# A two-layer graph network on one Trainium2 core: a shorter prelude, the last attention tiles side by side, and work of a step's start left for the next block

## The chip, the cores and the metric

The kernel runs on one core of a Trainium2 chip. The metric is the time on the device of one execution, in microseconds; three executions of the kernel before took 3805.06, 3805.78 and 3810.45 us, so the median is 3805.78 us. A profile is of one execution of its own. The engines are PE (matrix products and transposes through an identity, into PSUM), DVE (vector work), ACT (activations and most copies out of PSUM), POOL (elementwise work on SBUF, and here DMA issues too) and SP (which only issues DMAs). Each works through its own list of instructions in order and waits at semaphores for the others.

## What is computed

There are N = 2708 nodes with D = 512 features each, 22 tiles of up to 128 rows (the last has 20). Layer one is a graph attention with 8 heads of 64, layer two two steps of a diffusion with a "nucleus" attention. Cut to what matters:

```
h = relu(layernorm(x));  f = h W            # per head
e_self, e_neigh = f . a_self, f . a_neigh
attn = softmax(leaky(e_self[:,None] + e_neigh[None,:]) masked by adj)
x = x + relu(attn f + b)
X = relu(layernorm(x));  S = adj + I
for s in 0, 1:
    logits = (Xa W1) W2 (Xa W3)^T           # N x N
    A  = softmax(logits kept to the smallest set of largest terms with mass >= 0.9)
    Xf, Xb, Xa = Rf Xf, Rb Xb, A Xa         # Rf, Rb: S scaled by row, column sums
    Z += Xf U1[s] + Xb U2[s] + Xa U3[s]
x = x + layernorm(X + Z) gamma + beta
```

Since Rf and Rb are S with its rows scaled, the kernel multiplies by S and scales the result.

## The kernel before, in words

**Prelude** (lines 216 to 294). W, the attention vectors and the small weights are loaded; DVE forms `wa`, W times both attention vectors (L231, L232). Then a loop over 22 tiles: x is loaded (L254), normalised with `moments` (BN statistics on DVE, the power on POOL), centred on DVE (L257), clipped on POOL (L258), transposed on PE (L262), copied to `h_t` by ACT (L264). PE then forms `pe` (L270, 8 columns, e_neigh by node), `pr_t` (L273, e_self with heads as rows) and `pf` (L276, the features). ACT takes exponentials of them (L278 to L280), DVE writes the weighted features `fw` (L281). `r_t` holds e_self for all nodes and is written to DRAM (`en_d`, L284) at the end. The order of the instructions here and in layer one is made by a scheduler.

**Layer one** (L381 to L425). The nodes are cut into six chunks of 4, 4, 4, 4, 3 and 3 tiles. For each chunk and each group of four heads, over the 22 tiles of neighbours, DVE forms the attention terms `e` (L411) and PE accumulates them into `po` (L413). What remains for each tile of a chunk is a list of five stages (`finished`): `turned` (transposes of `o_t`), `shared` (division by the sums), `normed`, `cleared` (the second layer's normalised input, to `va_d`) and `asked` (its transposes, its split into a high and a low half, and its keys and queries to `kq_d`). These stages are put between the tiles of the next chunk's loop; those of the last chunk (tiles 19, 20, 21) come after it, tile after tile, in the order i*5+n (L420 to L425).

**The steps** (L883 on). The order on PE, ACT, DVE and SP is that of the source here; POOL's is the scheduler's. A step works on pairs of tiles, 11 blocks, with `g` from -1 to 10. Block g does four things at once:

- `search` finds for pair g+1 the threshold that keeps a mass of 0.9: rounds of passes over the 128 x 2708 exponentials on DVE (`mass`, L603), a choice (`choose`, L674 to L680), then `late()`, then `finish` (L779 on), which makes `keep` and ends with a branch (L863).
- `lg[g+2].products()` (L488) forms the logits of pair g+2 on PE; ACT copies them to `p` (L498). There are four buffers of `p`, so that of pair g+2 is free only when `finish` of pair g is done.
- `exp` (L501) is a list of steps on ACT, called fills: four exponentials over a whole row (L528, L535), on POOL the guesses (`points`, L538), twelve "looks" (L528, passes that count the mass above three guesses for each tile), and `masses` on POOL (L553), which the next search starts from.
- `late` runs, for pair g, `attended` (A Xa: transposes of `keep`, L983, copies `at`, L987, products L1002) and `mixed` (the products with U, L1030). Between their products `paced` places fills and "others".

The others (`part`, L913) are the products with S for four tiles (`product`, L938, with loads of `hl` and `s_r` by SP), and at their end `scaled`: ACT scales a result to `xe` (L944, two buffers), POOL writes it to `xfb_d`, and in step 0 DVE splits it in two halves (L181, L182) that POOL writes to DRAM too. `diffused` (L963) loads the scaled rows of pair g back.

In block -1 there is no pair to attend: `late` issues all fills, then all others, in that order, and only then does `finish` follow on DVE:

```
if g < 0:
    paced(fills, len(fills))
paced(others, len(others))
paced(fills, len(fills))
```

Of the kernel before, what the change touches and what calls it, by code (L numbers as in the profile page):

```python
# [9 lines left out]
F32 = mybir.dt.float32  # L10
# [14 lines left out]
P = 128  # L25
# [28 lines left out]
def kernel(  # L54
# [147 lines left out]
    with ExitStack() as l0:  # L202
# [13 lines left out]
        with tc.tile_pool(name="l0w", bufs=1) as wp, tc.tile_pool(name="l0p", bufs=2) as pp, \  # L216
                tc.tile_pool(name="l0ps", bufs=2, space=PSUM) as ps:
            w_sb = wp.tile([P, KD, D], F32, name="w_sb")
# [31 lines left out]
            r_t = wp.tile([H, N], F32, name="r_t")  # L250
            for t in range(NT):
                pr = rows[t]
                xt = pp.tile([P, D], F32, name="xt", bufs=3)
                nc.sync.dma_start(out=xt[:pr], in_=x[cols[t], :])  # L254
                h = pp.tile([P, D], F32, name="h")
                mean, rs = moments(pp, xt[:pr], pr)
                nc.vector.tensor_scalar(h[:pr], xt[:pr], mean, rs, op0=OP.subtract, op1=OP.mult)  # L257
                nc.gpsimd.tensor_scalar(h[:pr], h[:pr], 0.0, None, op0=OP.max)  # L258
                pt = ps.tile([P, KD, P], F32, name="tp")
                h_t = pp.tile([P, KD, P], F32, name="h_t")  # L260
                for k in range(KD):
                    nc.tensor.transpose(pt[:, k, :pr], h[:pr, k * P:(k + 1) * P], ident[:pr, :pr])  # L262
                for k in range(KD):
                    nc.scalar.activation(h_t[:, k, :pr], pt[:, k, :pr], AF.Copy,  # L264
                                         accum_out=hs[:, k, t:t + 1])
                pf = ps.tile([P, D], F32, name="pf")
                pe = ps.tile([P, H], F32, name="pe")
                pr_t = ps.tile([H, P], F32, name="pr_t")
                for k in range(KD):
                    nc.tensor.matmul(pe[:pr], lhsT=h_t[:, k, :pr], rhs=wa[:, k, H:],  # L270
                                     start=(k == 0), stop=(k == KD - 1))
                for k in range(KD):
                    nc.tensor.matmul(pr_t[:, :pr], lhsT=wa[:, k, :H], rhs=h_t[:, k, :pr],  # L273
                                     start=(k == 0), stop=(k == KD - 1))
                for k in range(KD):
                    nc.tensor.matmul(pf[:pr], lhsT=h_t[:, k, :pr], rhs=w_sb[:, k, :],  # L276
                                     start=(k == 0), stop=(k == KD - 1))
                nc.scalar.activation(fw[:pr, t, :, DH], pe[:pr], AF.Exp)  # L278
                nc.scalar.activation(kk[:pr, t, :], pe[:pr], AF.Exp, scale=-C)
                nc.scalar.activation(r_t[:, cols[t]], pr_t[:, :pr], AF.Exp, scale=C)  # L280
                nc.vector.tensor_mul(fw[:pr, t, :, :DH],  # L281
                                     pf[:pr].rearrange("p (h d) -> p h d", h=H),
                                     fw[:pr, t, :, DH:].to_broadcast([pr, H, DH]))
            nc.sync.dma_start(out=en_d, in_=r_t)  # L284
# [36 lines left out]
        def finished(t, o_t, c0):  # L321
# [5 lines left out]
            def turned():  # L327
                xt = work.tile([P, D], F32, name="xt0")
                nc.sync.dma_start(out=xt[:pr], in_=x[cols[t], :])
                held.append(xt)  # L330
                for g, grp in enumerate(hgroups):
                    pn = ps_t.tile([P, 512], F32, name=f"pn{g}")
                    pns.append(pn[:, :HG * DV].rearrange("p (h d) -> p h d", h=HG))
                    for i, hd in enumerate(grp):
                        nc.tensor.transpose(pns[g][:pr, i, :], o_t[:, hd, c0:c0 + pr], ident[:DV, :DV])

            def shared():
                den = small.tile([P, H], F32, name="den")
                rden = small.tile([P, H], F32, name="rden")
                o = work.tile([P, D], F32, name="o")  # L340
                held.append(o)
                o3 = o.rearrange("p (h d) -> p h d", h=H)
                for pn, grp in zip(pns, hgroups):
                    nc.vector.tensor_scalar(den[:pr, grp[0]:grp[-1] + 1], pn[:pr, :, DH],
                                            lone_n[:pr, t:t + 1], None, op0=OP.add)
                nc.vector.reciprocal(rden[:pr], den[:pr])
                for pn, grp in zip(pns, hgroups):
                    s = slice(grp[0], grp[-1] + 1)
                    nc.vector.scalar_tensor_tensor(o3[:pr, s, :], f3[:pr, s, :], lone[:pr, t:t + 1],
                                                   pn[:pr, :, :DH], op0=OP.mult, op1=OP.add)  # L350
                nc.gpsimd.tensor_mul(o3[:pr], o3[:pr], rden[:pr].unsqueeze(2).to_broadcast([pr, H, DH]))
                nc.gpsimd.tensor_add(o[:pr], o[:pr], b_b[:pr])
# [8 lines left out]
            def cleared():  # L361
                _, o, mean, rs = held
                v = work.tile([P, D], F32, name="v")
# [5 lines left out]
            def asked():  # L369
                v = held[4]  # L370
                pt = ps_t.tile([P, 512], F32, name="pn0").rearrange("p (k d) -> p k d", k=KD)
                for k in range(KD):
                    nc.tensor.transpose(pt[:, k, :pr], v[:pr, k * P:(k + 1) * P], ident[:pr, :pr])
                v_t = work.tile([P, KD, P], F32, name="v_t", bufs=1)
                nc.scalar.copy(v_t[:, :, :pr], pt[:, :, :pr])
                split_rows(halves, nc.gpsimd, v[:pr], t, vhl_d)
                project(halves, ps_t.tile([P, 512], F32, name="pn1"), v_t, t, 0)
# [4 lines left out]
        for ci, tiles in enumerate(tchunks):  # L382
# [22 lines left out]
            for grp, r_b in zip(hgroups, r_bs):  # L405
                po = [ps_o.tile([DV, 512], F32, name="po") for _ in grp]
# [12 lines left out]

            for i, t in enumerate(tiles):  # L420
                for n, stage in enumerate(finished(t, o_t, t * P - n0)):
                    later.setdefault(i * 5 + n, []).append(stage)
# [460 lines left out]
    for s in range(STEPS):  # L883
        last = s == STEPS - 1
        with ExitStack() as st:
# [28 lines left out]
            def part(half, b):  # L914
# [9 lines left out]
                if last or first:  # L924
                    half[:] = [ps_s.tile([P, D], F32, name=f"q{i}") for i in range(len(quad))]
# [4 lines left out]
                def product(c):  # L930
                    hl = sp.tile([P, 2, D], F32R, name="hl", bufs=3)
# [186 lines left out]
            with tc.manual_schedule(engines={PE, ACT, DVE, SP}):  # L1118
# [16 lines left out]
                ready = None  # L1135
                for g in range(-1, NP):

                    fills = []
                    if g + 2 < NP:
                        lg[g + 2].products()  # L1140
                    if g + 3 < NP:
# [4 lines left out]
                    others = part(half, g + 2)  # L1146
# [6 lines left out]
                    def late(g=g):  # L1153
                        if g >= 0:
                            keep, rden = ready
                            xf, xb = diffused(pairs[g])
                            xa, v_t = attended(pairs[g], keep, rden, fills, others, lambda: turned_rows(pairs[g], xf))
                            done.extend(mixed(pairs[g], v_t, xb, xa, others, fills))
                        elif last:
                            spread()  # L1160
                        if g < 0:
                            paced(fills, len(fills))
                        paced(others, len(others))
                        paced(fills, len(fills))
# [41 lines left out]
```

## Time and profile before

| what | us |
|---|---|
| median of three executions | 3805.78 |
| the profiled execution: its own time | 3807.19 |
| its span, first to last instruction | 3804.9 |
| prelude and the wait for layer one's first products | 0 to about 175 |
| layer one's loop | about 175 to 1082 |
| its last three tiles, to the first product of logits | 1082 to 1135 |
| step 0: block -1, blocks 0 to 10 | 1135 to 1293, to about 2400 |
| step 1: block -1, blocks 0 to 10 | about 2400 to 2569, to 3805 |

Over the span PE is busy 89%, DVE 69%, ACT 41% and POOL 22%; the mean granted TensorE clock is 0.957. Times in the text are microseconds from the start of the span. In an answer of the timeline, the columns are start, duration, engine, line, operation, output and inputs, a count where equal instructions were merged, and in brackets how long the engine had been idle and what it waited for. In the table by stretches each engine has its busy time and its number of instructions; the clock (1.00 is full speed), the DMA share and the DMA rate follow.

### The profile page before, as it was taken

To read this page: it belongs to the slowest core of one execution; us is meant where nothing else is said; L and a number is where in the kernel's file an instruction comes from. 1 tells how busy PE (TensorE), PEld (TensorE's weight loads), DVE (VectorE), ACT (ScalarE), POOL (GpSimd) and SP (SyncE) were. 2 spreads that over 40 slices of the span, in tenths; PEclk is the share of its full clock that TensorE was granted. 3 is DMA by queue.
4 is the path that set the end of the run, shared out by engine and by line. 5 is a ranking of instruction groups with operands and counts; after the bars stand their busy time and mean duration, and the time that the engine had idled before them with its cause. 6 is when DMAs were issued, how large, how long until landed. Compare 5 with 4: busy or idle time off the path is not lost. (4 is left out here: it accounts for less than half of the span.)

```text
span 3804.9 us, 35734 instructions
## 1 busy us (share of the span) xinstructions
PE 3402.3 (89%) x11313; PEld 1772.6 (47%) x11313; DVE 2611.5 (69%) x4814; ACT 1542.6 (41%) x2328; POOL 825.6 (22%) x1186
## 2 busy tenths in 40 slices
PE   7999999999955398999989899769999999999888
PEld 4433333333434254555555453445555665556442
DVE  3387888889945644545364642698779798777991
ACT  2234211111116255666656541256545556445511
POOL 3202331514331112121211211311121211211101
PEclk9999999999978699999999999989999999999999
DMA  2277434233226345453544543684566665567552
GB/s 75 80 265 260 156 99 139 82 106 108 82 66 234 135 147 191 152 203 113 198 153 152 188 153 97 224 291 164 188 209 220 228 211 190 198 208 245 182 204 70
DMA packets 276122, 634.09 MB, mean 167 GB/s; under 512 B 37033, under 2 KB 70097, under 8 KB 272899
## 3 DMA queue, kind: packets, MB, share of 16 engines
q1 hardware_dynamic: 248847, 540.99, 43.2%
q0 software_dynamic: 27024, 90.30, 6.2%
q8 instruction: 90, 1.47, 0.2%
q14 instruction: 161, 1.32, 0.1%
HBM read 509.07 MB, written 122.10 MB: 166 GB/s over the span
## 5 line engine op out<-in xcount | busy, mean ns | idle before, releaser
L1002 PE MATMUL a<-va,at 128*128 128x512 f32 (+2 forms) x1936 | 889.0, 598 | 10.2 <-ACT at L987 10.1
L938 PE MATMUL q<-hl,s_r 128*128 128x512 f32 x2904 | 824.2, 430 | 53.3 <-DMA s_r<-s_d 52.9
L413 PE MATMUL po<-e,fw 128*65 128x512 f32 (+4 forms) x2112 | 841.1, 554 | 29.9 <-DVE e L411 17.3
L411 DVE SCALAR_TENSOR_TENSOR e<-r_b,kk,a_c 128x512 f32<-128x512 f32 (+4 forms) x1056 | 752.5, 741 | 68.7 <-PE po L413 18.9
L938 PEld LDWEIGHTS q<-hl,s_r 128*128 128x128 f32 x2904 | 546.5, 190 | 298.7 <-issue 140.4
L528 ACT ACTIVATE junk_a<-p,nth 128x2708 uint8<-128x2708 f32 (+1 forms) x240 | 613.1, 2555 | 93.3 <-POOL nth L548 89.7
L413 PEld LDWEIGHTS po<-e,fw 128*65 128x65 f32 (+1 forms) x2112 | 286.4, 140 | 545.1 <-issue 272.9
L1002 PEld LDWEIGHTS a<-va,at 128*128 128x128 f32 (+2 forms) x1936 | 336.5, 186 | 374.0 <-issue 340.4
L1030 PE MATMUL a<-u_k,v_t 128*128 128x512 f32 (+1 forms) x1056 | 489.4, 599 | 23.1 <-ACT xa L1010 15.5
L603 DVE SCALAR_TENSOR_TENSOR junk<-p,th 128x2708 bf16<-128x2708 f32 (+1 forms) x132 | 402.3, 3048 | 4.0
L987 ACT COPY at<-t 128x512 f32<-128x512 f32 (+3 forms) x308 | 139.9, 475 | 440.9 <-PE t L983 440.5
L496 PE MATMUL t<-keys,q_t 128*128 128x452 f32 x528 | 168.1, 447 | 167.0 <-ACT p L498 155.0
L1030 PEld LDWEIGHTS a<-u_k,v_t 128*128 128x128 f32 (+1 forms) x1056 | 187.6, 186 | 242.0 <-issue 182.6
L779 DVE SCALAR_TENSOR_TENSOR keep<-p,th 128x2708 f32<-128x2708 f32 (+1 forms) x44 | 133.4, 3033 | 143.0 <-PE t L983 141.8
L181 DVE TENSOR_SCALAR split_hl<-xe 128x512 int32<-128x512 int32 (+1 forms) x44 | 19.0, 433 | 306.4 <-ACT xe L944 247.3
L496 PEld LDWEIGHTS t<-keys,q_t 128*128 128x128 f32 x528 | 92.6, 213 | 237.9 <-ACT p L498 208.0
L781 DVE MAX8 vn<-keep 128x8 f32<-128x2708 f32 (+1 forms) x66 | 196.8, 2981 | 2.3
L498 ACT COPY p<-t 128x452 f32<-128x452 f32 (+2 forms) x264 | 132.0, 539 | 144.0 <-DVEq L863 71.2
L395 ACT ACTIVATE s_c<-a_c 128x512 fp32r<-128x512 f32 (+3 forms) x132 | 76.2, 577 | 253.1 <-DMA a_c<-in_adj_t_dram 129.4
L983 PE MATMUL t<-ident,keep 128*128 128x128 f32 (+1 forms) x968 | 147.3, 274 | 24.3 <-DVE keep L731 16.6
L983 PEld LDWEIGHTS t<-ident,keep 128*128 128x128 f32 (+1 forms) x968 | 115.1, 139 | 104.2 <-issue 75.9
L523 DVE TENSOR_REDUCE nmx<-p 128x1 f32<-128x2708 f32 (+1 forms) x44 | 129.2, 2966 | 26.7 <-ACT p L498 26.7
(281 smaller groups left out, 3134.1 us busy)
## 6 DMA issues: line engine op xcount, KB each, us to landing
s_r<-s_d SPq DMA_DIRECT2D x330, 256.0 KB, 4.0
hl<-vhl_d SPq DMA_DIRECT2D x132, 512.0 KB, 4.0
u_k<-in_L_gnn_U_dram SPq DMA_DIRECT2D x264, 256.0 KB, 4.9
hl<-fhl_d SPq DMA_DIRECT2D x132, 512.0 KB, 5.3
hl<-bhl_d SPq DMA_DIRECT2D x132, 512.0 KB, 3.6
arow<-in_adj_dram SPq DMA_DIRECT2D x21, 1354.0 KB, 7.1
s_d<-s_c SPq DMA_DIRECT2D x88, 256.0 KB, 2.4
a_c<-in_adj_t_dram SPq DMA_DIRECT2D x84, 256.0 KB, 3.9
```

Of the source, the lines that this page charges most:

```text
L411: nc.vector.scalar_tensor_tensor(e[:pr, :cw], r_b[:pr, i, :cw], kk[:pr, t, hd:hd + 1], a_c[t][:pr, :cw], op0=OP.max, op1=OP.mult)
L413: nc.tensor.matmul(po[i][:, :cw], lhsT=fw[:pr, t, hd, :], rhs=e[:pr, :cw], start=(t == 0), stop=(t == NT - 1))
L496: nc.tensor.matmul(pl[:, :c1 - c0], lhsT=q[:, i], rhs=self.keys[:, c0:c1], start=(i == 0), stop=(i == 1))
L528: nc.scalar.activation(junk[:pr], self.p[i][:pr], func, **kw)
L603: v.scalar_tensor_tensor(junk_b[:pr], ps_[i][:pr], th, ps_[i][:pr], op0=OP.is_ge, op1=OP.mult, accum_out=dst)
L779: v.scalar_tensor_tensor(keep[i][:pr], ps_[i][:pr], t, ps_[i][:pr], op0=OP.is_lt, op1=OP.mult, accum_out=left[:pr, i:i + 1] if e else None)
L781: v.max(vs, keep[i][:pr])
L938: nc.tensor.matmul(half[j], lhsT=s_r[:, j * P:(j + 1) * P], rhs=hl[:, h], start=(c == 0 and h == 0), stop=(c == NT - 1 and h == 1))
L983: nc.tensor.transpose(pt[:rows[c], j, :pr], keep[i][:pr, cols[c]], ident[:pr, :pr])
L987: nc.scalar.copy(at[:r, j0:j1, :pr], pt[:r, j0:j1, :pr])
L1002: nc.tensor.matmul(pa[:pr], lhsT=at[:rows[c], j, :pr], rhs=va[:rows[c], c, :], start=(c == 0), stop=(c == NT - 1))
L1030: nc.tensor.matmul(pz[i][:rows[t]], lhsT=v_t[i][:, k, :rows[t]], rhs=u_k, start=(n == 0 and k == 0), stop=(n == 2 and k == KD - 1))
```

## The change

Prelude: the normalisation of a tile is a function of its own, `cleared`, called two tiles ahead (the first two before the weights are loaded). `pe` has 16 columns, both attention terms by node, and `pf` comes before it. The `pr_t` products are gone: ACT copies e_self of four tiles into `es`, PE transposes it once for four tiles, ACT takes the exponential, and SP writes it tile by tile to `en_d`.

Layer one: the stages of the last chunk's tiles are in the order n: all three tiles' `turned`, then all `shared`, and so on. They use the six `po` banks; `xt0`, `o` and `v` have three buffers and `v_t` two.

The steps: block -1 issues 5 + G*NA = 11 fills (the four exponentials, the points and six looks) and only the products of the others (11 in step 0, 22 in step 1). The other six looks and `masses` go to block 0, after its logits' products and before everything else of it. The scaled results (8 in step 0, 4 in step 1) stand first in the others of block 0, and `diffused` is after them as one of the others; from block 1 on it is run at the start of `late`, as before. The PSUM tiles of a part are taken at its first product.

```
 # prelude, per tile
+                h = hts[t]
 ...
+                if t + 2 < NT:
+                    hts.append(cleared(t + 2))
 ...
-                pe = ps.tile([P, H], F32, name="pe")
-                pr_t = ps.tile([H, P], F32, name="pr_t")
-                for k in range(KD):
-                    nc.tensor.matmul(pe[:pr], lhsT=h_t[:, k, :pr], rhs=wa[:, k, H:],
-                                     start=(k == 0), stop=(k == KD - 1))
-                for k in range(KD):
-                    nc.tensor.matmul(pr_t[:, :pr], lhsT=wa[:, k, :H], rhs=h_t[:, k, :pr],
-                                     start=(k == 0), stop=(k == KD - 1))
+                pe = ps.tile([P, 2 * H], F32, name="pe")
                 for k in range(KD):
                     nc.tensor.matmul(pf[:pr], lhsT=h_t[:, k, :pr], rhs=w_sb[:, k, :],
                                      start=(k == 0), stop=(k == KD - 1))
+                for k in range(KD):
+                    nc.tensor.matmul(pe[:pr], lhsT=h_t[:, k, :pr], rhs=wa[:, k, :],
+                                     start=(k == 0), stop=(k == KD - 1))
 ...
+                nc.scalar.copy(es[:pr, t % TG, :], pe[:pr, :H])
+                if t % TG == TG - 1 or t == NT - 1:
+                    pr_t = ps.tile([TG * H, P], F32, name="pr_t")
+                    nc.tensor.transpose(pr_t, es.rearrange("p t h -> p (t h)"), ident)
+                    r_t = pp.tile([TG * H, P], F32, name="r_t")
+                    nc.scalar.activation(r_t, pr_t, AF.Exp, scale=C)
+                    for j in range(t % TG + 1):
+                        c = t - t % TG + j
+                        nc.sync.dma_start(out=en_d[:, cols[c]], in_=r_t[j * H:(j + 1) * H, :rows[c]])
 ...
 # layer one, after a chunk
+            final = ci == len(tchunks) - 1
             for i, t in enumerate(tiles):
-                for n, stage in enumerate(finished(t, o_t, t * P - n0)):
-                    later.setdefault(i * 5 + n, []).append(stage)
+                if final:
+                    bank = lambda g: ps_o.tile([P, 512], F32, name="po")
+                else:
+                    bank = lambda g: ps_t.tile([P, 512], F32, name=f"pn{g}")
+                for n, stage in enumerate(finished(t, o_t, t * P - n0, bank)):
+                    later.setdefault(n if final else i * 5 + n, []).append(stage)
 ...
 # the steps
+                looks, left = [], []
                 for g in range(-1, NP):
                     fills = []
                     if g + 2 < NP:
                         lg[g + 2].products()
+                    paced(looks, len(looks))
 ...
-                    others = part(half, g + 2)
+                    rows_in = []
+                    if g >= 0:
+                        left.append(lambda g=g: rows_in.extend(diffused(pairs[g])))
+                    others = left + part(half, g + 2)
+                    left = []
 ...
                         if g >= 0:
                             keep, rden = ready
-                            xf, xb = diffused(pairs[g])
-                            xa, v_t = attended(pairs[g], keep, rden, fills, others, lambda: turned_rows(pairs[g], xf))
-                            done.extend(mixed(pairs[g], v_t, xb, xa, others, fills))
-                        elif last:
+                            if g:
+                                paced(others, 1)
+                            xa, v_t = attended(pairs[g], keep, rden, fills, others, lambda: turned_rows(pairs[g], rows_in[0]))
+                            done.extend(mixed(pairs[g], v_t, rows_in[1], xa, others, fills))
+                            paced(others, len(others))
+                            paced(fills, len(fills))
+                            return
+                        if last:
                             spread()
-                        if g < 0:
-                            paced(fills, len(fills))
-                        paced(others, len(others))
-                        paced(fills, len(fills))
+                        paced(fills, 5 + G * NA)
+                        paced(others, NT if last else NT - NT // 2)
+                        looks.extend(fills)
+                        left.extend(others)
```

## The prediction

> **What bounds the kernel now.** I read the table by stretches first, since the mean of 89% busy PE hides where PE is not the bound.
>
> ```profile
> 0.00:170.00 170.00, 144.66 (x632) 81.05 (x633) 53.56 (x118) 36.77 (x245) 52.33 (x72) 1.00 0.19 51
> 1082.00:1135.00 53.00, 12.43 (x63) 10.02 (x62) 12.48 (x35) 5.09 (x14) 29.08 (x41) 0.52 0.29 90
> 1205.00:1294.00 89.00, 12.49 (x46) 9.19 (x45) 31.90 (x60) 37.80 (x34) 11.35 (x28) 0.59 0.41 143
> 2400.00:2569.00 169.00, 115.22 (x433) 79.59 (x433) 153.11 (x233) 74.84 (x90) 40.36 (x37) 0.89 0.84 279
> ```
>
> The columns after the length are PE, weight loads, DVE, ACT and POOL. The prelude is PE's after a start of 27 us without it. In layer one's last tiles nobody is busy: POOL with 29 of 53 us leads a chain. In step 0's block -1 all stand still in turn. In step 1's block -1 DVE is busy 153 of 169 us: it is the bound there. So the two steps begin differently, and the same edit meets two situations. The timeline of both block ends shows it; first step 0, DVE and then ACT:
>
> ```profile
> 1204.58 0.16 DVE L680 TENSOR_TENSOR th<-th 128x2 f32<-128x2 f32 x1
> 1240.09 0.43 DVE L181 TENSOR_SCALAR split_hl<-xe 128x512 int32<-128x512 int32 x1 [35.35 <-ACT xe L944]
> ...
> 1267.28 3.03 DVE L779 SCALAR_TENSOR_TENSOR keep<-p,th 128x2708 f32<-128x2708 f32 x1
> ```
>
> ```profile
> 1239.30 0.19 ACT L528 ACTIVATION_READ_ACCUMULATOR junk_a<-p,nth 128x1 f32 x1
> 1239.39 0.67 ACT L944 ACTIVATE xe<-q,rinv 128x512 f32<-128x512 f32 x1
> ...
> 1293.16 0.97 ACT L498 COPY p<-t 128x452 f32<-128x452 f32 x2 [29.73 <-DVEq L863]
> ```
>
> DVE has chosen at 1204.7, but the splits of the scaled results stand before `finish` in its list; they wait for ACT's twelve looks and then for buffers, until 1267.3. The copies to `p` wait for `finish`. In step 1 it is otherwise:
>
> ```profile
> 2543.55 0.19 ACT L528 ACTIVATION_READ_ACCUMULATOR junk_a<-p,nth 128x1 f32 x1
> 2557.26 1.27 ACT L944 ACTIVATE xe<-q,cinv 128x512 f32<-128x512 f32 x2 [13.53 <-PE q L938]
> ...
> 2569.17 0.97 ACT L498 COPY p<-t 128x452 f32<-128x452 f32 x2 [6.88 <-DVEq L863]
> ```
>
> All looks are done 25.6 us before `finish` lets the copies go: there they cost nothing.
>
> [...] (ACT stood 29.73 us at one copy). So where a moved instruction lands in a list matters more than its length. [...] the clock is 0.65 over 1294 to 1302, after the long wait, and 1.00 from 1302 on. [...] so SP will stand at the loads of `diffused`.
>
> **Prelude.** PE's rows from 100.65 to 113.23 are two tiles, 12.58 us: transposes 1.12, `pe` and `pr_t` in turns 2.53 (held by ACT's copies), `pf` 3.54, `pe` 0.88, `pr_t` 0.97, `pf` 3.54. Afterwards: 1.12 + 2 x (3.54 + 0.88) = 9.96; 16 columns instead of 8 change nothing visible[...]. That is 2.62 less for a pair, 26.2 for 20 tiles. ACT's copies are hidden behind `pf`. Six transposes of `es` come back at some 0.27 each, 1.6. At the start, tile 0's products end at 36.1 (L276 begins at 32.6); `wa` is ready at 21.9. With the normalisation done ahead only `pe` of tile 0 needs `wa`; two x loads ahead of W on SP push it by 2 x 0.45, so to 22.8, and tile 0 ends at 23.8: 12.3 gained. Tile 3's normalisation comes after `wa` on DVE and its clip (1.6) after tile 2's on POOL, at about 30, some 1.3 late. Sum 12.3 + 26.2 - 1.6 - 1.3 = 36 us. The `en_d` writes on SP stand ahead of later x loads, but those wait for `xt` buffers freed only later; the last ones lie under the sum `hsum` (3.7). Per tile DVE needs 2.1, POOL 2.5 and ACT 1.7, all under 4.98. Bounds 28 and 40. In layer one's loop the lists of PE and DVE are the same as before: 0.
>
> **Last three tiles.** One tile after another takes 14.6 us (L373 at 1091.6, 1106.2, 1121.7), of which POOL works about 9.7. Side by side POOL has all three without a gap: from 1084.1, 3 x (1.1 + 1.26 + 1.26 + 0.6 + 0.81 + 0.64 + 1.28 + 0.56 + 1.5 + 0.71), less a short last split of keys, plus two memsets, 1.4, is 30 us; small gaps between (0.08 each, 0.3 before each DMA) add 3. It ends at 1117.3 rather than 1127.4: 10 us, bounds 6 and 13. The load of the keys and queries (1127 to 1134.7) keeps its length.
>
> **Step 0.** `finish` starts at 1204.7 and lasts as before, 1293.2 - 1267.3 = 25.9: copies at 1230.6, ended 9.1 later, 1239.7. ACT has done six looks by 1223.5, so nothing waits. Then six looks, 6 x 2.68 = 16.1, in front of the first `at` copy: PE begins `attended` at 1256.5 instead of 1303.2, 46.7 ahead, and `masses` let DVE start at 1256.8 instead of 1297.6. Now comes the new wait. Scaled results stand between the `at` copies: the third `xe` needs the first one's buffer, which DVE's split frees, and DVE's splits come after its choice, 26.5 us into the search: 1283.3 + 1.15 = 1284.5. Behind that `xe` on ACT is the `at` copy of the fifth group; PE runs four groups (to 1272) and stands until 1285.8. Then for four groups ACT carries 0.6 + 2 x 2.7 + 0.7 to 1.4 (copy, fills, scaling) = 6.7 to 7.4, where PE has 3.9 and no products to fill it: PE ends the group of the eighth `at` at about 1314 and, with 2 products of 1.87 in each of the last four, the attention at 1343.5, two products still owed (3.7). Before, it ended at 1367.8. Lead 1367.8 - 1343.5 - 3.7 = 20.6; PE comes to it cold twice, some 2.5. Gain 18 us; bounds 0 (each scaled result at its old pace, eight in 27 us) and 44 (no wait after 1256.5). DVE's `finish` of this block ends near 1349, PE's block near 1380: covered by 30. `x` needs only the first four scaled results, landed near 1295, so the loads behind it are in time.
>
> **Step 1.** Nothing is gained ahead of 2569.2, which DVE sets. The six looks, hidden before, now follow the copies (end 2578.5): 16.1 later, and PE begins at 2595.3 instead of 2579.4: -15.9. It stood 17 us, so it starts at half clock: -2. Four scaled results and `diffused` go into the second tile's groups; the first product's loads stand behind `diffused` on SP, which waits for the second result's write, and ACT places them after its fills; they land near 2632 where PE is free at 2624.4: -7. DVE starts 19.5 later, in a block of 117 us where it needs about 98, so it just keeps up. Loss 25 us; bounds 14 and 34.
>
> **Sum.** 36 + 10 + 18 - 25 = 39 us. On the profiled 3807.2 (span 3804.9, 2.3 around it) that is 3768.2; the median lies 1.4 lower: 3766.
>
> **Rivals.** (1) Step 0 keeps its whole lead: ACT catches up while PE does the products. 36 + 10 + 42 - 18 = 70: 3736. For it: before, the same fills fit under PE. Against: the list puts the third scaling ahead of the fifth copy, and DVE cannot be there earlier. (2) The starts give nothing: step 0's scaled results take their old pace and step 1's loss is at its end. 36 + 10 + 0 - 33 = 13: 3793. For it: 8.47 us gaps among the splits at 1260. Against: those are DMA waits when eight come at once. (3) The prelude is not shortened by the products, since the chain x load, statistics, power, clip (2.3 + 0.9 + 0.8 + 0.55 + 1.6 = 6.2) runs once for each tile instead of three deep. 12 + 10 + 18 - 25 = 15: 3791. Against: three buffers, 6.2 / 3. (4) The slower side: a prelude without gaps makes the granted clock fall in layer one's loop. Its 906 us run at 0.97; each hundredth costs 9.3 us, so from 0.93 on the gain is gone; at 0.92, 3812. Against: 1.00 over 110 to 160 us with PE busy 99%. That the change does nothing is excluded in the prelude, where instructions go.
>
> **Numbers.** The case worked out 0.62 (its own range 3752 to 3780), rival 1 0.13, rivals 2 and 3 together 0.17, rival 4 and its like 0.05, no net change 0.03. The range reaches through most of rivals 1 to 3: 3738 to 3793. Below 0.2% (7.6 us) a measurement of this kernel can't tell a change; faster 0.92, same 0.03, slower 0.05.
>
> **What will show it.** Layer one's first `e` near 139 rather than 175; no `pr_t` products by tile; the first logits about 46 ahead of 1134.7. In step 0, DVE's `keep` right after its choice, ACT waiting at a scaling for DVE (about 19 us), the first U product 64 to 70 ahead of 1367.8. In step 1 POOL's `signs` after the copies, and the lead down by 23 to 27 from one end of its block -1 to the other of block 0. Wrong, if ACT's scaling doesn't wait, if the clock in the loop leaves 0.97, or if the lead at 2400 is not near 64.

## The result, and the profile after

The changed kernel takes 3775.99 us, the median of four executions (3772.09 to 3781.52), against 3805.99 us for the kernel before (3805.06 to 3810.45): a ratio of 0.992, with a 95% interval of 0.9903 to 0.9937. It is 30 us faster. The forecast was 3766 us, 39 us faster. The measured time lies in the forecast's own range, but two of its four terms came out just beyond their bounds (the last tiles gave 5.5 us, the start of step 1 took 36.7), and the errors partly cancel: that the sum came so near is in part luck. The profiled execution took 3774.21 us with a span of 3772.1 us, 32.8 us shorter than before.

To see where the gain arises and where it goes, I read the start of the same work in both traces. The lead is the time before minus the time after.

| start of | before | after | lead | lead by the prediction |
|---|---|---|---|---|
| layer one's first `e` | 175.1 | 140.3 | 34.8 | 36 |
| the last product of layer one's loop | 1081.9 | 1046.6 | 35.3 | 36 |
| the first logits | 1134.7 | 1093.9 | 40.8 | 46 |
| step 0: first product of A Xa | 1303.2 | 1215.6 | 87.6 | 92.7 |
| step 0: first U product | 1367.8 | 1303.2 | 64.6 | 64 |
| step 0: last U product | 2385.2 | 2321.1 | 64.1 | 64 |
| step 1: first product of A Xa | 2579.4 | 2531.6 | 47.8 | 48 |
| step 1: first U product | 2645.7 | 2620.8 | 24.9 | 39 |
| the end | 3804.9 | 3772.1 | 32.8 | 39 |

The table by stretches of the changed kernel, for the stages that the prediction showed of the kernel before (length, PE, weight loads, DVE, ACT, POOL, PE's clock, DMA share, GB/s):

```profile
0.00:140.00 140.00, 117.88 (x466) 66.91 (x466) 54.12 (x119) 34.87 (x252) 51.99 (x73) 0.99 0.27 82
1047.00:1094.00 47.00, 11.17 (x62) 9.67 (x62) 15.14 (x35) 4.71 (x13) 30.27 (x41) 0.51 0.34 101
1164.00:1191.00 27.00, 9.48 (x33) 6.80 (x31) 23.20 (x45) 16.30 (x13) 4.65 (x10) 0.75 0.25 77
2336.00:2506.00 170.00, 115.81 (x433) 79.97 (x433) 153.11 (x233) 56.35 (x74) 37.52 (x30) 0.89 0.78 260
```

From DVE's choice in step 0's block -1 to the first copy of the logits it is 27 us now, where it was 89, and DVE works in 23 of them. Step 1's block -1 is as long as it was (169 and 170 us) and DVE is busy in it for the same 153.11 us: nothing was to be gained there. The last tiles take 47 us instead of 53, with POOL as busy as before.

Step 0, DVE's timeline (start, length, engine, line, operation, in brackets the idle time before it and what ended it):

```profile
1163.96 0.16 DVE L701 TENSOR_TENSOR th<-th 128x2 f32<-128x2 f32 x1
1164.15 3.04 DVE L800 SCALAR_TENSOR_TENSOR keep<-p,th 128x2708 f32<-128x2708 f32 x1
...
1242.40 0.43 DVE L181 TENSOR_SCALAR split_hl<-xe 128x512 int32<-128x512 int32 x1
```

and ACT's in the same block:

```profile
1226.68 0.59 ACT L1008 COPY at<-t 128x512 f32<-128x512 f32 x1 [2.70 <-PE t L1004]
1243.64 0.69 ACT L965 ACTIVATE xe<-q,rinv 128x512 f32<-128x512 f32 x1 [16.38 <-DVE split_hl L182]
1244.23 0.58 ACT L1008 COPY at<-t 128x512 f32<-128x512 f32 x1
```

`keep` follows the choice at once. The halves of the scaled results now follow the next choice, and there the predicted wait stands: ACT waits 16.38 us at the third scaled result. PE stands behind it for the copy at 1244.23:

```profile
1233.73 0.38 PE L1004 MATMUL t<-ident,keep 128*128 128x128 f32 x2
1244.86 5.73 PE L1023 MATMUL a<-va,at 128*128 128x512 f32 x8 [10.74 <-ACT at L1008]
```

Step 1, first ACT, then POOL, SP's DMA queue and PE:

```profile
2559.96 1.26 ACT L965 ACTIVATE xe<-q,cinv 128x512 f32<-128x512 f32 x2
2571.38 0.69 ACT L965 ACTIVATE xe<-q,cinv 128x512 f32<-128x512 f32 x1 [10.16 <-DMA xfb_d<-xe]
...
2577.67 0.67 ACT L965 ACTIVATE xe<-q,cinv 128x512 f32<-128x512 f32 x1
```

```profile
2556.55 1.49 POOL L562 TENSOR_TENSOR x<-half,powers 128x2 f32<-128x2 f32 x1 [24.64 <-ACT junk_a L549]
2560.14 0.69 POOL L561 TENSOR_TENSOR x<-tot,powers 128x2 f32<-128x2 f32 x1 [2.10 <-ACT p L556]
2560.92 2.50 POOL L570 TENSOR_SCALAR thr<-tot 128x2 f32<-128x2 f32 x1
2563.49 3.00 POOL L571 TENSOR_SCALAR top<-tot 128x2 f32<-128x2 f32 x1
...
2568.88 0.65 POOL L966 DMA_DIRECT2D xfb_d<-xe  x1
```

```profile
2487.86 87.32 SPq L989 DMA_DIRECT2D x<-xfb_d  x4
2575.28 0.38 SPq L953 DMA_DIRECT2D hl<-fhl_d  x1
```

```profile
2559.28 3.60 PE L1023 MATMUL a<-va,at 128*128 128x512 f32 x8
2579.97 3.75 PE L959 MATMUL q<-hl,s_r 128*128 128x512 f32 x8 [17.09 <-DMA s_r<-s_d]
```

The chain is to be read from its end. PE stands 17.09 us for the first loads of the product with S. SP issues them at 2575.28, since the four loads of x (L989) hold its queue from 2487.86 on. The loads wait for the writes of the scaled results (84.3 us in two waits, the longer 81.2). The first of these is ready on ACT at about 2560.6, but POOL issues its write only at 2568.88, because the guesses for the next pair (L561 to L571) stand ahead of it in POOL's list: it goes out 8.3 us after its data is there. And because that write is late, the third scaled result waits 10.16 us for its buffer.

The guesses themselves are held up by DVE. L570 and L571 work on two elements a partition and took 2.50 and 3.00 us, where their medians in this trace are 0.25 and 0.22. Each ended less than 0.1 us after a pass of DVE's search that had begun before it:

```profile
2560.29 3.04 DVE L624 SCALAR_TENSOR_TENSOR junk<-p,th 128x2708 bf16<-128x2708 f32 x1
...
2563.37 3.04 DVE L624 SCALAR_TENSOR_TENSOR junk<-p,th 128x2708 bf16<-128x2708 f32 x1
```

By these numbers some 5 of the 8.3 us are DVE's (an estimate: the two durations less the two medians); the last section has more on it.

The last three tiles of layer one, POOL:

```profile
1076.02 0.69 POOL L173 DMA_DIRECT2D kq_d<-kq_hl  x1 [0.29 <-POOL kq_hl L172]
1077.35 0.95 POOL L180 MEMSET split_hl<- 128x1024 f32 x1 [0.64 <-DMA vhl_d<-split_hl]
1083.64 0.31 POOL L164 MEMSET kq_hl<- 128x256 f32 x1 [5.34 <-DMA kq_d<-kq_hl]
...
1086.91 0.69 POOL L173 DMA_DIRECT2D kq_d<-kq_hl  x1 [0.29 <-POOL kq_hl L172]
```

The third tile's halves wait 5.34 us for the second tile's write to land. That write was slow: it was issued at 1076.02 and landed 7.6 us later, while the first tile's, of the same size, took 2.5. Between the two SP had begun to load the keys (two loads of 640 KB at once, two small ones at the end):

```profile
1073.78 16.45 SPq L924 DMA_DIRECT2D keys<-kq_d  x4
```

### The profile page after: what moved, and what is told of

Same layout as the page of the kernel before. It is cut to its first block, busy times and chain, and to the rows that moved or that the text cites. A ratio compares the mean times of both kernels' runs of the same rounds, so it can differ in the third digit from the quotient of the medians.

```text
span 3772.1 us, 35425 instructions
## 1 busy us (share of the span) xinstructions
PE 3383.3 (90%) x11143; PEld 1760.6 (47%) x11143; DVE 2611.1 (69%) x4814; ACT 1540.1 (41%) x2334; POOL 838.2 (22%) x1187
## 5 line engine op out<-in xcount | busy, mean ns | idle before, releaser
L1023 PE MATMUL a<-va,at 128*128 128x512 f32 (+2 forms) x1936 | 898.0, 603 | 58.0 <-ACT at L1008 57.9
L624 DVE SCALAR_TENSOR_TENSOR junk<-p,th 128x2708 bf16<-128x2708 f32 (+1 forms) x132 | 402.2, 3047 | 4.0
L800 DVE SCALAR_TENSOR_TENSOR keep<-p,th 128x2708 f32<-128x2708 f32 (+1 forms) x44 | 133.4, 3033 | 132.4 <-PE t L1004 131.1
L802 DVE MAX8 vn<-keep 128x8 f32<-128x2708 f32 (+1 forms) x66 | 196.8, 2981 | 2.3
```

The lines of the kernel that those rows point to most:

```text
L624: v.scalar_tensor_tensor(junk_b[:pr], ps_[i][:pr], th, ps_[i][:pr], op0=OP.is_ge, op1=OP.mult, accum_out=dst)
L800: v.scalar_tensor_tensor(keep[i][:pr], ps_[i][:pr], t, ps_[i][:pr], op0=OP.is_lt, op1=OP.mult, accum_out=left[:pr, i:i + 1] if e else None)
L802: v.max(vs, keep[i][:pr])
L1023: nc.tensor.matmul(pa[:pr], lhsT=at[:rows[c], j, :pr], rhs=va[:rows[c], c, :], start=(c == 0), stop=(c == NT - 1))
```

## The experiments

My theory after the result: the prelude gives 35 us that pass through to the end, the last tiles 5, the start of step 0 some 24, and the start of step 1 takes 37 of these back. The rivals are that a lead is lost somewhere in any case, or that another engine sets the end. Beside each group of variants the kernel before ran on the same chip; its medians were 3804.16, 3806.93 and 3806.36 us, and each ratio below is against the one of its group.

### The prelude alone, and the prelude with the last tiles

The first kernel is the one before with the new prelude only; the second is the changed kernel with both steps' starts as before:

```
-  paced(fills, 5 + G * NA)
-  paced(others, NT if last else NT - NT // 2)
+  paced(fills, len(fills))
+  paced(others, len(others))
   # diffused at the start of late in block 0 too
-  if g:
+  if True:
```

> The kernel before with the new prelude alone. My theory reads the gain by landmarks: the prelude gives 35 us at layer one's first e, and a lead of the whole kernel is carried to the end, since every engine is earlier by the same amount. So first e at 140, first logits near 1099, end 33 to 36 us ahead of before: 3770 to 3773 us. That would be as fast as the whole change, so the last tiles and the starts of the steps together would be worth nothing. Rival: part of the prelude's lead is lost later (at the end of layer one or at the steps' starts), and the other parts make up for it: 3780 to 3795 us.

> The changed kernel with both steps' starts as before: new prelude and the last tiles side by side alone. My theory: the lead of 40 us at the first logits goes through to the end: 3763 to 3766 us, so leaving work at the steps' starts, as the change does it, costs some 10 us in all (24 gained in step 0, 37 lost in step 1, some of it made up at the end). Rival: the starts as before eat some of the lead: 3770 to 3776 us.

The prelude alone took 3767.47 us (ratio 0.9899, 0.9883 to 0.9916), with the last tiles 3765.7 us (0.9891, 0.9868 to 0.9914). The prelude alone is 2.5 us below the range that I had given for it. In the traces their leads are 34.9 and 34.3 us at layer one's first product and 37.1 and 40.0 at the end. So the lead passes through to the end, and the prelude alone is worth at least as much as the whole change: what the change does at the starts of the steps costs some 10 us in sum (3775.99 - 3765.7; the two intervals just overlap). The leads are not constant on the way: in layer one's loop, where PE's and DVE's lists are the same, they shift by up to 6 us from kernel to kernel, and by up to 7 in step 0. From differences of that size between the ends of two traces I read nothing; a short stretch that several traces repeat is another matter.

### Two buffers for the halves in layer one

```
-  halves = l0.enter_context(tc.tile_pool(name="l0halves", bufs=1))
+  halves = l0.enter_context(tc.tile_pool(name="l0halves", bufs=2))
```

> The changed kernel with two buffers instead of one for the halves that POOL writes (split_hl, kq_b, kq_hl) in layer one. My theory: the last three tiles side by side gave 5.4 us instead of 10 because the third tile's halves wait for the write of the second one's (POOL's memset of kq_hl stands 5.34 us, that of split_hl 0.64); with two buffers POOL does not stand, the first logits come some 5 us earlier (near 1089), and the time is near 3771 us. Rival: the writes' own landing is what the load of the keys waits for, whoever issues them when: first logits at 1093 or 1094 as now, 3776 us.

It took 3773.87 us (0.9924, 0.9906 to 0.9943): no difference to the changed kernel that the time can show. POOL's waits are gone in its trace:

```profile
1078.97 0.39 POOL L164 MEMSET kq_hl<- 128x256 f32 x1
...
1081.14 0.68 POOL L173 DMA_DIRECT2D kq_d<-kq_hl  x1 [0.29 <-POOL kq_hl L172]
```

From the end of the loop to the first logits the lead grows by 8.6 us (33.8 to 42.4) instead of 5.5 (35.3 to 40.8). The gain of this stretch repeats: it is 5.2 to 6.2 us in the nine traces of kernels with the tiles side by side and one buffer, and 8.6 to 8.7 in the two with two buffers (this one and the combination below). The last write goes out 5.8 us earlier, but the logits follow it by 11.1 us rather than 7.0. Theory and rival each hold in part: the buffer explains 3 of the missing 4.5 us. What is left is the landing: the last write, issued 3.6 us after SP began its loads of the keys, now takes 6.2 us to land, where in the changed kernel it took 2.2.

### Step 0: looks and scaled results apart

These kernels have step 1's start as before (see below), so that only step 0 differs. "Scaled only" leaves the scaled results for block 0 and places all twelve looks in block -1; "looks only" does the reverse (with `diffused` again at the start of block 0); a third keeps step 0 as changed and gives the scaled results four buffers:

```
   # scaled only
-  paced(fills, 5 + G * NA)
+  paced(fills, len(fills))
   # looks only
-  paced(others, NT if last else NT - NT // 2)
+  paced(others, len(others))
   # four buffers
-  x = work.tile([P, D], F32, name="xe")
+  x = work.tile([P, D], F32, name="xe", bufs=2 if last else 4)
```

> Step 1's start as before (as in the run that took 3742.4 us), and in step 0 only the scaled results are left for block 0; all twelve looks stand in block -1. My theory: the six looks left cost step 0 too. Without them VectorE gets its masses some 13 us earlier, so its choice, and behind it the halving that the third scaled result on ScalarE waits for, comes 13 us earlier; ScalarE does 12 looks to 1201.5, then the copies of the logits, so the first attended product comes 0 to 5 us earlier, the stand of 10.7 us at the fifth group goes, and the first U product comes 9 to 14 us earlier: 3728 to 3733 us. Rival: the copies of the logits, 11 us later, push everything: 3742 us or more.

> Step 1's start as before, and in step 0 only the six looks are left for block 0; the scaled results stay in block -1 and their halves stand ahead of keep on VectorE, as before. My theory: the gain of step 0 (24 us) comes from the scaled results, not from the looks: the eight scaled results take their 27 us ahead of keep, starting when six looks are done (1185 instead of 1201 in the clock of the changed kernel), then keep, copies and six looks: first attended product near 1263, first U product near 1327, 3762 to 3769 us. Rival: six looks less ahead of the halves are the gain: 3742 to 3748 us.

> Step 1's start as before, step 0 as in the change, but with four buffers for the scaled results in step 0 instead of two. My theory: ScalarE's wait of 16.4 us at the third scaled result for VectorE's halving goes, since only the fifth needs a buffer back; TensorE's stand of 10.7 us at the fifth group goes with it, but two fills for each group then set the pace: the first U product 5 to 10 us earlier, 3732 to 3737 us. Rival: ScalarE's fills, which need the row maxima that VectorE makes only at 1232, are the bound: no change, 3742 us.

| left in step 0 (step 1 as before) | us | ratio, 95% | gain from the first logits to the first U product |
|---|---|---|---|
| nothing | 3765.7 | 0.9868 to 0.9914 | -2.3 |
| looks | 3765.78 | 0.9873 to 0.9906 | -1.4 |
| looks and scaled results | 3742.38 | 0.9822 to 0.9854 | 23.4 |
| looks and scaled results, four buffers | 3728.98 | 0.9779 to 0.9812 | 35.3 |
| scaled results | 3728.66 | 0.9779 to 0.9811 | 37.4 |

The gain of step 0 comes with the scaled results. Leaving looks gains nothing by itself: with looks only, the eight scaled results take their old pace, which is that of DMA waits, and hold `keep` back; ACT's timeline shows it:

```profile
1208.95 0.69 ACT L965 ACTIVATE xe<-q,rinv 128x512 f32<-128x512 f32 x1 [11.10 <-DMA xfb_d<-xe]
1210.37 0.69 ACT L965 ACTIVATE xe<-q,cinv 128x512 f32<-128x512 f32 x1 [0.73 <-DMA xfb_d<-xe]
1241.31 0.97 ACT L519 COPY p<-t 128x452 f32<-128x452 f32 x2 [30.26 <-DVEq L884]
```

And beside the scaled results the looks cost 13.7 us (3742.38 - 3728.66). They delay `masses`, so DVE's search, so the halves behind its choice. With scaled results only, the last step of DVE's choice (L701) begins at 1233.24 instead of 1242.22, although the first logits of that kernel came 4.6 us later than the changed kernel's, and ACT's wait at the third scaled result shrinks from 16.38 to 9.84 us:

```profile
1234.66 0.69 ACT L965 ACTIVATE xe<-q,rinv 128x512 f32<-128x512 f32 x1 [9.84 <-DVE split_hl L182]
```

With four buffers it is the fifth result that waits, and it waits 1.34 us:

```profile
1247.03 0.69 ACT L965 ACTIVATE xe<-q,rinv 128x512 f32<-128x512 f32 x1 [1.34 <-DVE split_hl L182]
```

With four buffers nothing else changes in step 0, so the wait at the third scaled result cost the change some 13 us there. I had expected less of the buffers (3732 to 3737). That leaving no looks gains the same 13 us has more than one cause: PE's stand at the fifth group falls from 10.74 to 4.20 us, and PE comes to the first product of A Xa straight from the logits, so that eight products take 3.70 us instead of 6.72.

### Step 1: looks and scaled results apart

```
   # step 1 as before
-  if g:
+  if g or last:
+  paced(fills, len(fills) if last else 5 + G * NA)
+  paced(others, len(others) if last else NT - NT // 2)
   # looks only: without the line of fills; scaled only: with the line of fills alone
```

> The changed kernel with step 1's block -1 as before: all looks, all products and scaled results there; step 0 leaves them as in the change. My theory: the lead of 64 us at the end of step 0 (2321.1 against 2385.2 for the last U product) goes through step 1's start, which took 37 us of it: first attended product of step 1 at 2515, its first U product near 2582; time 3740 to 3746 us. Rival: step 1 gives the lead back in any case (VectorE has 98 of 117 us per block, or memory is late): 3765 to 3776 us.

> The changed kernel, but in step 1 only the six looks are left for block 0; the scaled results stay in block -1. My theory: the loss of 37 us in step 1 is 16 for the six looks ahead of the first copy of keep's transposes, some 2 for a cold TensorE, and 19 for the scaled results: their writes stand on POOL behind the next pair's guesses, the loads of x on SP behind those writes, and the first loads for the product with S behind them (TensorE stood 17.1 us there). So here the loss is 16 to 20 and the time 3756 to 3760 us. Rival A: the looks make nearly all of it, by way of masses and VectorE's late search: 3770 to 3776. Rival B: the looks cost nothing, since TensorE catches up: 3740 to 3746.

> The changed kernel, but in step 1 all twelve looks stand in block -1 and only the scaled results are left for block 0: the fourth case beside none left (3742), looks alone (3762) and both (3776). My theory: the scaled results cost some 15 to 20 us by themselves, since their writes stand on POOL behind the guesses of the next pair, and these wait for exponentials that ScalarE does only from the fourth group on: TensorE again stands near 17 us at the first product with S; 3757 to 3762 us. Rival: without the looks the guesses are early enough, and the scaled results cost little: 3742 to 3748 us.

| left in step 1 (step 0 as changed) | us | ratio, 95% | lead at the last U product of step 0, and at the end |
|---|---|---|---|
| nothing | 3742.38 | 0.9822 to 0.9854 | 65.8, 65.1 |
| looks | 3762.45 | 0.9873 to 0.9906 | 62.1, 44.7 |
| scaled results | 3760.5 | 0.9848 to 0.9891 | 65.6, 45.0 |
| both (the changed kernel) | 3775.99 | 0.9903 to 0.9937 | 64.1, 32.8 |

In step 1 each of the two costs 18 to 20 us, and both together 34; with the looks the time is 2 us above the range that I had given. The rival that the lead is given back in any case is out: with step 1 as before, all of it reaches the end. Without the looks the first product of A Xa comes at a lead of 65, so the 16 us there are theirs. With scaled results only, POOL's list holds the write back as in the changed kernel,

```profile
2540.77 3.32 POOL L561 TENSOR_TENSOR x<-tot,powers 128x2 f32<-128x2 f32 x1 [2.88 <-ACT p L556]
...
2552.49 0.65 POOL L966 DMA_DIRECT2D xfb_d<-xe  x1
```

(its result was ready at about 2541.2), and PE stands for the loads behind it:

```profile
2562.90 3.75 PE L959 MATMUL q<-hl,s_r 128*128 128x512 f32 x8 [19.39 <-DMA s_r<-s_d]
```

### Step 1: the writes issued by ACT

If POOL's list is the cause, writes that don't stand in it must remove the wait:

```
-  nc.gpsimd.dma_start(out=xfb_d[i, cols[t], :], in_=x[:pr])
+  (nc.scalar if last and b == 1 else nc.gpsimd).dma_start(out=xfb_d[i, cols[t], :], in_=x[:pr])
```

> The changed kernel, but the four scaled results of step 1's start are written by DMAs that ScalarE issues right behind each, instead of POOL. My theory: POOL's list is the cause of TensorE's stand of 17.1 us at the first product with S (the first write is issued 8.9 us after its result is there, 2568.9 against 2560.0; the third scaled result waits for its buffer, the loads of x for the writes). Here the writes go out at once, the stand shrinks to 2 to 5 us, and the time to 3761 to 3766 us. Rival: the stand comes from ScalarE's looks and from the loads' own time: stand near 15 us, 3774 to 3776 us.

It took 3773.84 us (0.9908, 0.9888 to 0.9929), no clear gain, and my expectation failed. The writes do go out at once, 0.7 us after each result begins (in the changed kernel it was 8.9 us after the first began, 8.3 after it was ready), and SP's first loads for the product follow at 2561.70 instead of 2575.28. ACT and PE:

```profile
2560.49 0.69 ACT L965 ACTIVATE xe<-q,cinv 128x512 f32<-128x512 f32 x1 [1.29 <-DMA xfb_d<-xe]
...
2567.17 2.55 ACT L549 ACTIVATE junk_a<-p,nth 128x2708 uint8<-128x2708 f32 x1 [4.98 <-POOL nth L569]
...
2572.40 0.67 ACT L965 ACTIVATE xe<-q,cinv 128x512 f32<-128x512 f32 x1
```

```profile
2567.49 2.90 PE L959 MATMUL q<-hl,s_r 128*128 128x512 f32 x6 [7.18 <-DMA s_r<-s_d]
2573.12 0.73 PE L959 MATMUL q<-hl,s_r 128*128 128x512 f32 x2 [2.73 <-ACT xe L965]
```

PE's stand falls from 17.09 to 7.18 and 2.73 us. What is left has two causes: the loads go out only at 2561.70, behind the write that SP waits for, while PE is free from 2560.3 on; and the fourth scaled result stands on ACT behind two looks, which wait 4.98 us for the guesses on POOL (two of them, of 2.99 and 3.00 us, again end with DVE's passes), while the product needs the PSUM bank that this scaling frees. After the first block of a step its lead stays nearly constant; the loss from step 0's last U product to there falls from 36.7 us (64.1 to 27.4) to 32.9 (66.4 to 33.5). So POOL's list held the writes, but it is not shown to be the cause of the loss: with its link removed the next ones of the chain hold most of the time. What the links are worth one by one is not settled; the cost of the scaled results as a whole (18 to 20 us) is.

### A combination

New prelude, last tiles side by side with two buffers for the halves, in step 0 the scaled results only, with four buffers, and step 1 as before:

> A version meant to beat both: the new prelude, the last tiles side by side with two buffers for the halves, step 1's start as before, in step 0 only the scaled results left, with four buffers for them. My theory adds the parts to the 3742 us of step 1 as before: 3 us from the last tiles, 9 to 14 from the looks, up to 3 more from the buffers: 3722 to 3730 us. Rival: the looks and the buffers remove one and the same wait and ScalarE's own work sets the pace behind it: 3730 to 3735 us.

It took 3719.57 us (3717.12 to 3727.6), a ratio of 0.9777 (0.976 to 0.9794): 87 us faster than before and 56 faster than the changed kernel, and 9 faster than either of the two ways of step 0 alone. I had expected 3722 to 3730 us. In its trace the stretch from the first logits to the first U product gains 43.0 us, so the two ways of step 0 add up in part; what of the 9 us is theirs and what is layer one's I can't separate. ACT's wait for DVE is gone; what is left there is a wait for POOL's guesses:

```profile
1232.70 0.67 ACT L965 ACTIVATE xe<-q,rinv 128x512 f32<-128x512 f32 x1
1233.28 0.57 ACT L1008 COPY at<-t 128x512 f32<-128x512 f32 x1
1239.93 2.55 ACT L549 ACTIVATE junk_a<-p,nth 128x2708 uint8<-128x2708 f32 x1 [6.08 <-POOL nth L569]
```

## Why the prediction was right, and where it was not

The time forecast was 10 us too low (its own sum comes to 3766.8; and for a clock of 0.92 its fourth rival should have read 3816, not 3812). By the table of leads: prelude -1.2, last tiles -4.5 with 0.5 from the loop between, step 0 +5.3, step 1 -11.7, the end +5.4; 39 with these is 32.8. The loss in step 1 was half as large again as forecast, and 5.3 us more than forecast in step 0 and 5.4 at the end made up for most of the excess: the mechanisms were largely right, but the closeness of the sum owes something to luck.

**Prelude: right.** It gave 34.8 us for 36. Two tiles take 9.8 us (the features' products of every second tile begin at 94.6 and 104.4) for a predicted 9.96; the first tile's begin at 19.8 instead of 32.6, 12.8 earlier for 12.3. The chain of the normalisation does not bound it, so the third rival is out. The prediction took `pe` with 16 columns to cost what it cost with 8, which was my estimate; in the traces one of its products takes 252 ns on average with 16 columns and 260 with 8 (168 of each).

**Last tiles: mechanism right, a wait overlooked.** They gave 5.5 us for 10, just outside the bounds. The step that failed is the list of POOL's work "without a gap": three tiles close together want a buffer each for their halves, and there is one. In the kernel before, the tile ahead was 14.6 us away and its write had long landed. Nor did the prediction see that SP's first loads of the keys now begin between the tiles' writes; the write that followed their start took 7.6 us to land.

**Step 0: mechanism right, size a little low.** 23.3 us for 18. The third scaled result waits on ACT for DVE (16.4 us for 19), PE stands (10.7 for 13.8), and then ACT sets the pace: the next four copies of `at` follow each other by 6.5, 6.3, 8.6 and 6.9 us where 6.7 to 7.4 were said (in the 8.6 ACT waits 4.37 us for POOL's guesses). The term that was mis-sized is the 2.5 us for PE's starts behind a wait, where the prediction calls PE cold: at granted clocks of 0.63 and 0.59 (over 1244.86 to 1250.42 and 1257.69 to 1263.66) eight products take 5.73 and 6.13 us instead of 3.60, but where ACT needs 6.3 or more for each group this costs nothing. The rest is that PE's group of the eighth copy ended 3.7 us earlier than worked out. The experiments add what the prediction did not weigh: it counted the six looks ahead of the first copy of `at` and of `masses`, as the change has them, but did not ask whether leaving them gains anything. With all twelve in block -1 the first product of A Xa comes no later (a lead of 87.0 against 84.2 with step 1 as before in both), and step 0 gains some 14 us more.

**Step 1: half right.** The loss is 36.7 us for 25. The six looks cost 16.3 us at the first product for a predicted 15.9, and the start behind PE's wait of 15.73 us 2.1 for 2: eight products take 5.78 us where 3.7 is usual, with a granted clock of 0.50 from 2531.6 to 2533.5, 0.69 on average from there to 2537.2, and 1.00 over 2536 to 2538. The 2 us were my estimate; the half clock is in the trace of the kernel before too, 0.50 over 1294 to 1298, behind the wait for `finish`, and 1.00 over 1300 to 1310. The step that failed is "they land near 2632 where PE is free at 2624.4: -7". In the times of the kernel before they landed at 2644, and PE stood 17.1 us. I had followed SP's queue behind the write, but not the write itself: it is issued by POOL, and POOL's list has the next pair's guesses ahead of it, which wait for exponentials on ACT and then for DVE's passes. In the trace 8.9 us pass from the end of the exponential at 2559.98 to the write at 2568.88, filled with the guesses that stand ahead of it. The prediction had followed the lists of ACT and DVE, and not POOL's. That SP stands at the loads of `diffused` was right: the kernel before has it (35.0 us in two waits for the writes to `xfb_d`, over 1200 to 1300), and the changed one too, with 84.3. DVE, 19 us late at its choice (lead 63.2 at the copies, 44.2 at the choice), kept up as said.

**The end.** In the profile of the changed kernel the last three blocks gain 5.4 us more (27.4 to 32.8): PE waits 1.50 us for DVE ahead of the last pair's transposes instead of 4.69, and the clock granted for its first eight products is 1.00 (3.70 us), where in the kernel before it is 0.50 for the transposes and 0.64 for the products (5.64 us). The variant with writes by ACT waits 4.70 us there and shows no such gain (33.5 to 33.4). Why the wait is short in one profile and not in the other is open; in the medians the whole gain is 30 us, not 32.8.

**Rivals.** That step 0 keeps its whole lead was wrong for the change as made, but 35 to 43 us were to be had there, as that rival had it (42), once the wait was removed. That the starts give nothing is close to the truth for their sum (-10 us), by another mechanism: a gain and a larger loss. The clock in layer one's loop did not fall (0.98 over 150 to 1040 us, 0.97 before).

## What to carry to other kernels

When work is moved behind a point where an engine waits, follow it through every list that it touches: the engine that makes it, the one that issues its write, the queue of the load that reads it, and the buffer or bank that its successor needs. The same edit gained 23 us in the step where the moved work had stood ahead of the bound, and lost 34 to 37 in the step where it had been hidden under it; so such an edit is to be priced for each place where it acts, and made only where it pays. Two kinds of work moved by one edit are to be tried apart: here one of them brought the gain of step 0, and the other took over a third of it away.

## What was unexpected of the hardware

**POOL's small operations stand while DVE passes over a row.** In the changed kernel's trace 42 of POOL's operations on two or six elements a partition began within one of DVE's passes over rows of 2708 (L624, L731, L733, L800, L1119). They took 0.59 to 3.09 us, and each ended 0.05 to 0.11 us after the pass. Seven more began within 0.05 us of the start of a pass and took 0.22 to 0.25 us, as did the 15 that began under MAX8 (L802, also 3 us long; 0.20 to 0.25), and 222 with no DVE operation longer than 0.3 us beside them took 0.20 to 0.26. Powers (L561, L562) are not among these; the 13 that began within a pass took 0.86 to 3.15 us and ended 0.55 to 0.58 us after it. Other traces repeat it: in that of the kernel before, 39 operations took 0.72 to 3.09 us and ended 0.05 to 0.11 us after a pass, and with scaled results only in step 1, L561 took 3.32 us, L567 2.87 and L568 3.00, and the write came behind them. So an engine's short work can be priced only together with what another engine does at that time. What the two engines share, and why MAX8 does not hold POOL, these runs do not show.

**Some small writes land late, and always in the same place.** In all thirteen traces the write that POOL issues 1.8 to 2.4 us after SP began its loads of the keys (two of 640 KB) lands 6.8 to 7.7 us after its issue (7.34 in the kernel before, 7.57 in the changed one), while of the writes that were issued in the 10 us before that load, up to half a microsecond ahead of it, none took more than 4.7. DVE's passes are not the reason: in the changed kernel it works for 0.41 us between 1073.5 and 1084. That the loads are the cause is likely but not shown: no kernel here moved them.
